# A planner with pauses: steps fed by another engine drawn behind a set amount of other work, k times v one step later, queries ahead of the spreading

## The chip, the cores and the metric

One core of one Trainium2 chip runs the whole program. The metric is the device time of one launch in microseconds (us). Before the change it is 5066.79 us, the median of 3 runs (5059.32 to 5072.86).

## The reference

The input is x, 8 images of 384 channels on 32 by 32 pixels, all in fp32. Four layers follow one another; only the first two are touched by the change.

```python
# layer 0, per image; both directions of the sequence of 1024 pixels
xn   = rmsnorm(x)                              # over the 384 channels
u, z = split(xn @ in_proj)                     # 384 -> 768
u    = silu(conv1d(u))                         # 4 taps, depthwise
dt, B, C = split(u @ x_proj)                   # 24, 16, 16
delta = softplus(dt @ dt_proj + b)
h[t] = exp(delta*A)*h[t-1] + delta*u*B         # 384 channels x 16 states
y    = (sum_n h*C + u*D) * silu(z)
x1   = x + 0.5*(0.25*(fwd + bwd) @ out_proj + sigmoid(dwconv3x3(xn))*xn)
# layer 1, per image
h = c2(bn2(dwconv3x3(c1(bn1(x1))))) + x1       # c1, c2: 384 -> 384
q, k, v = split(qkv(h)); phi(t) = exp(0.5*(2t - t*t))
out = phi(q) @ (phi(k)^T v) / (phi(q) . sum phi(k))   # 8 heads of 48
h = h + proj(out)
x2 = h + mlp(layernorm(h))                     # 384 -> 1536 -> 384
# layer 2: seven depthwise convolutions (sum); layer 3: 1x1, 13x13 depthwise, gelu
```

## The kernel before, in words

**Stages.** An image is 1024 pixels in two halves of 512, with channels in NC = 3 groups of 128 partitions. For an image b there are three routines. `front(b)` makes what the scan reads: the norm (squares, a mean over channels by matmul `ms_s`, a reciprocal root `ms_r` on ScalarE, its spreading over partitions by matmul `ms_b`, the product `xn` on VectorE), the input projection `in` with weights `win`, the 3x3 gate `lc`, the 1-d convolution `c`, then `xd` and `dt`. `scan(b)` is the recurrence. `layer1(b)` is the output projection `op` and all of layer 1: `h`, `dw`, `c2`, k and v with their product `kvs`, the key sum and its spreading (`kss`, `kvp`), queries `q`, denominator `den` with its reciprocal `rz` and the spreading `rzb`, projection `pj`, layernorm (`mu`, `var_s`, `var_r`, `var_b`) and the MLP (`mf`, `mo`). At the end of all images come the two 13x13 convolutions with a pointwise product between (L330, L376), which the change does not touch.

**The scan.** It has 48 rounds in an image: 12 units (direction, half, channel group) of NR = 4. In each round ScalarE makes four exponentials `da` (L846), VectorE two products `du` (L851) and four recurrences `hs` (L863), GpSimd two products with C (L872), and TensorE sums the result with four matmuls into `acc` (L552 and L557, the line of a helper that all column-tiled products share). `hs` has 8 buffers, two a round, so VectorE may be four rounds ahead of TensorE; `da` has 4. The eight scans run one after the other, and the other two routines are dealt out between the rounds: while image b is scanned, `layer1(b-1)` and `front(b+1)` are.

**What sets the order.** Each routine is a Python generator that issues some instructions and yields the cost of what it just issued, about the TensorE time in us. A planner (L1194 to L1221) keeps a list of jobs [generator, total cost, first round, last round, cost done]. After each scan round it draws from the job that is furthest behind an even pace until none is behind. `front(b)` counts 100 units, paced from 8 rounds before the end of the scan two images earlier to 9 before the end of the last one; `layer1(b)` counts 310 over the 48 rounds of the next image. The order in which the program is written gives the priority; a scheduler then orders each engine's instructions by it[...]. Steps with a `defer` come one or more draws later (L527). Two helpers, `together` and `col32` (L547, L559), keep groups of matmuls together.

**Where the steps are written.** `front`: xi loads L639, squares L643, `rsqrt_mean` (L608) and `spread_rows` (L622), xn L650, win L658, t3 (the taps of lc) L673, lc L678, conv1d L707, xd L718, dt L736. `layer1`: kvs L1025, the k/v projections L1011, kv L1030, kss L1040, kvp L1054, wq L1061, q L1072, den L1080, rz L1085 to L1087, rzb L1092, pj L1098, mu L1106, var L1113 to L1132, MLP L1153 to L1180. Pools that matter: PSUM "mm" (`psum`) has 2 buffers, "mo" (`long_psum`) 3; `t2` 9, `a6` 7, weights `w` 4, images of rows `im` 8 in SBUF.

Of the kernel before, what the change touches and what calls it, by code (L numbers as in the profile page):

```python
# [11 lines left out]
AF = mybir.ActivationFunctionType  # L12
# [4 lines left out]
P = 128  # L17
# [390 lines left out]
def _layers01(tc, nc, B, xv, x2_d, dram, ident, mean_w, eps5, eps6, one, half, minus1, vec, bns, bnt,  # L408
# [12 lines left out]
    with ExitStack() as ctx:  # L421
# [84 lines left out]
        def t2(name):  # L506
            return sp.tile([P, HALF], FP, tag="t2", name=name, bufs=N_T2)
# [61 lines left out]
        def rows(t):  # L569
            return t.rearrange("p (h w) -> p h w", w=W)  # L570
# [51 lines left out]
        def spread_rows(r, name):  # L622
            ps = psum(f"{name}_b")
            for j in range(4):
                nc.tensor.matmul(
                    ps[:, j * P : (j + 1) * P], spread[:, j, :], r, start=True, stop=True,
                    skip_group_check=True,
                )
            return ps
# [2 lines left out]

        def front(b):

            xn = []
            for h in range(2):
                cols = bass.ts(h, HALF)
                xh = a6(f"xi_{b}_{h}")
                nc.sync.dma_start(xh, xv[b][:, :, cols])  # L639
                yield 0  # L640
                sqs = [t2(f"sq_{b}_{c}_{h}") for c in range(NC)]
                for c in range(NC):
                    nc.scalar.activation(sqs[c], xh[:, c, :], AF.Square)  # L643
                yield 0
                r = rsqrt_mean(sqs, eps6, f"ms_{b}_{h}")
                yield 1
                rstd = spread_rows(r, f"ms_{b}_{h}")
                t, mid = image6(f"xn_{b}_{h}")
                for c in range(NC):
                    nc.vector.scalar_tensor_tensor(  # L650
                        mid[c], rows(xh[:, c, :]), vec("norm_w", c), rows(rstd), ALU.mult, ALU.mult
                    )
                put_image(xn_d, b % 2, h, t, nc.gpsimd)
                xn.append(mid)
                yield 2
            uo = u_d[b % 2].rearrange("(c p) i -> p c i", p=P)
            for e in range(2):
                w = wtile(inproj_t[:, e * C : (e + 1) * C], f"win_{b}_{e}")  # L658
                for h in range(2):
                    for m in range(NC):  # L660
                        ps = psum(f"in_{b}_{e}_{m}_{h}")
                        dense(ps, w, m, xn[h])
                        t = t2(f"uz_{b}_{e}_{h}_{m}")
                        if e == 0:
                            nc.scalar.copy(t, ps)
                            nc.scalar.dma_start(uo[:, m, 3 + h * HALF : 3 + (h + 1) * HALF], t)
                        else:
                            nc.scalar.activation(t, ps, AF.Silu)
                            nc.scalar.dma_start(zv[b][:, m, bass.ts(h, HALF)], t)
                        yield 3  # L670


            t3 = tapw(taps3, f"t3_{b}")  # L673
            for h in range(2):
                for c in range(NC):
                    xr = t2(f"xr_{b}_{h}_{c}")
                    nc.sync.dma_start(xr, xv[b][:, c, bass.ts(h, HALF)])
                    ps = conv3(rows3(xn_d, b % 2, h, c, f"lc_{b}_{h}_{c}"), c, t3, f"lc_{b}_{h}_{c}")  # L678
                    lc = t2(f"lg_{b}_{c}_{h}")
                    nc.scalar.activation(lc, ps, AF.Tanh, bias=dwh[:, c, :], scale=0.5)  # L680

                    def local(h=h, c=c, lc=lc, xr=xr):
                        nc.vector.scalar_tensor_tensor(
                            rows(lc), rows(lc), one, xn[h][c], ALU.add, ALU.mult
                        )
                        nc.vector.scalar_tensor_tensor(xr, lc, rsh, xr, ALU.mult, ALU.add)
                        nc.gpsimd.dma_start(x1v[b][:, c, bass.ts(h, HALF)], xr)

                    defer(1, local)
                    yield 3  # L690


            for h in range(2):
# [33 lines left out]
                for d in range(2):  # L727
                    lo = 64 * d + DTR
                    nc.scalar.dma_start(bc_d[b, d][:, cols], xd[lo : lo + 2 * NST, :])
                yield 3  # L730
                for c in range(NC):
                    dls = []
                    for d in range(2):
# [209 lines left out]
        def layer1(b):  # L943
# [43 lines left out]
            for h in range(2):  # L987
# [13 lines left out]
                kvs[: PR + 1, 0:C], zero[:, 0 : PR + 1], zero[:, 0:C], start=True, stop=False,  # L1001
                skip_group_check=True,
            )
            for t in range(L // P):
                h, q = divmod(t, HALF // P)
                pix = xx[h][:, :, q * P : (q + 1) * P]
                kp, vt = t2(f"kp_{b}_{t}"), t2(f"vt_{b}_{t}")
                for w, dst in ((wk, kp), (wv, vt)):
                    ps = psum(f"kv_{b}_{t}_{dst.name}")
                    for k in range(NC):  # L1010
                        nc.tensor.matmul(  # L1011
                            ps[:, :C], pix[:, k, :], w[:, k, :], start=(k == 0), stop=(k == NC - 1)
                        )
                    if w is wk:
                        phi(kp[:, :C], ps[:, :C], f"k_{b}_{t}")
                    else:
                        vv1 = vt[:, : C + NPR].rearrange("p (a e) -> p a e", e=PR + 1)
                        nc.scalar.copy(vv1[:, :, PR : PR + 1], ones)
                        nc.scalar.copy(
                            vv1[:, :, 0:PR], ps[:, :C].rearrange("p (a e) -> p a e", e=PR)  # L1020
                        )
                last = t == L // P - 1
                for a in range(NPR):
                    s = slice(a * PR, (a + 1) * PR)
                    nc.tensor.matmul(  # L1025
                        kvs[: PR + 1, s], vv1[:, a, :], kp[:, s], start=False, stop=last,
                        skip_group_check=True,
                    )
                yield 6
            kv = t2(f"kv_{b}")  # L1030
            nc.vector.tensor_mul(
                kv[:PR, :C].rearrange("p (a e) -> p a e", e=PR),
# [2 lines left out]
            )  # L1035

            nc.scalar.copy(kv[PR : PR + 1, :C], kvs[PR : PR + 1, :C])
            kss = psum(f"kss_{b}")
            for c in range(NC):
                nc.tensor.matmul(  # L1040
# [12 lines left out]
            for a in range(NPR):  # L1053
# [4 lines left out]
                t = t2(f"kvp_{b}_{a}")  # L1058
                nc.scalar.copy(t[:PR, :C], ps[:PR, :C])
                nc.scalar.dma_start(kvp_d[b % 2, a * PR : (a + 1) * PR, :], t[:PR, :C])  # L1060
            wq = wtile(qkv_t[:, 0:C], f"wq_{b}")  # L1061
            kvp = wtile(kvp_d[b % 2], f"kvw_{b}")
            yield 4


            qps, xns = [], []
            for h in range(2):
                qp = a6(f"qp_{b}_{h}")
                qps.append(qp)
                for m in range(NC):  # L1070
                    ps = long_psum(f"q_{b}_{h}_{m}")
                    dense(ps, wq, m, xx[h])  # L1072
                    phi(qp[:, m, :], ps, f"q_{b}_{h}_{m}")
                    yield 3

            den, rz = long_psum(f"den_{b}"), t2(f"rz_{b}")
            ats = [slice(32, 64), slice(96, 128)]
# [7 lines left out]
                nc.scalar.activation(rz[at, :], den[at, :], AF.Ln, bias=eps6[at])  # L1085
            for at in ats:
                nc.scalar.activation(rz[at, :], rz[at, :], AF.Exp, scale=-1.0)  # L1087
            yield 3
            for k in range(NC):
                for h, at in enumerate(ats):  # L1090
                    ps = long_psum(f"rzb_{b}_{h}_{k}")
# [29 lines left out]
                    nc.vector.tensor_mul(xns[h][:, k, :], xns[h][:, k, :], rstd)  # L1121

            sq = squares(0)
            yield 0
            r0 = rsqrt_mean(sq, eps5, f"var_{b}_0")
            sq = squares(1)
            yield 1
            r1 = rsqrt_mean(sq, eps5, f"var_{b}_1")
            scaled(0, r0)
            yield 3  # L1130
            scaled(1, r1)
            yield 2  # L1132

            behind_gelu = []

# [55 lines left out]
        seconds = [layer1(b) for b in range(B)]  # L1191


        jobs = [[fold(), 36, 0, rounds, 0], [prepare, 7, 0, rounds, 0]]  # L1194
        for b in range(1, B):
            jobs.append([front(b), 100, max(0, (b - 1) * rounds - 8), b * rounds - 8 - 1, 0])
        for b in range(B - 1):
            jobs.append([seconds[b], 310, (b + 1) * rounds + 0, (b + 2) * rounds + 0, 0])
        for b in range(B):
            for i, _ in enumerate(scan(b)):  # L1200
                tick()
                if i == rounds:
                    break
                at = b * rounds + i
                if i == rounds - 8:
                    next(seconds[b])

                while True:
                    due = [
                        (w[4] / w[1] - (at + 1 - w[2]) / (w[3] - w[2]) if at + 1 < w[3] else -1, n)  # L1210
                        for n, w in enumerate(jobs) if w[2] <= at
                    ]
                    if not due or min(due)[0] >= 0:
                        break
                    w = jobs[min(due)[1]]
                    cost = next(w[0], None)
                    if cost is None:
                        jobs.remove(w)
                    else:
                        w[4] += cost  # L1220
        tick(everything=True)  # L1221

        scan_ctx.close()
# [95 lines left out]
```

## Time and profile before

| what | value |
|---|---|
| time, median of 3 runs | 5066.79 us (5059.32 to 5072.86) |
| span of the profiled execution | 5036.6 us |
| mean granted clock of TensorE | 0.906 |
| TensorE busy | 4203.6 us, 83% of the span |
| VectorE busy | 3791.7 us, 75% |
| GpSimd busy | 2997.3 us, 60% |
| ScalarE busy | 2637.3 us, 52% |
| front(0) alone | 0 to about 147 us |
| scans of images 0 to 7 begin | 150.8, 674.5, 1160.9, 1662.6, 2165.5, 2666.5, 3165.4, 3653.3 us |
| last scan ends | 4087.9 us |
| layer1(7) alone, with the windows' loads | to about 4490 us |
| convolutions and the product between | to 5036.6 us |

The page gives no other time of the profiled execution than its span, 30.2 us below the median of the runs. Times of engines are sums of instruction durations in that one execution. [...] In the views of waits a line reads "who waited for whom: us in all, times, longest"; in the views of windows, each row is a stretch of the span with the busy time and count of every engine, the granted clock, the share of the DMA engines and GB/s. "acc k" below is the sum of scan round k, counted from 0 in each image; what lies between acc k and acc k+1 in TensorE's list is what the other two routines do there.

### The profile page before, as it was taken

To read this page: it belongs to the slowest core of one execution; us is meant where nothing else is said; L and a number is where in the kernel's file an instruction comes from. 1 tells how busy PE (TensorE), PEld (TensorE's weight loads), DVE (VectorE), ACT (ScalarE), POOL (GpSimd) and SP (SyncE) were. 2 spreads that over 40 slices of the span, in tenths; PEclk is the share of its full clock that TensorE was granted. 3 is DMA by queue.
4 is the path that set the end of the run, shared out by engine and by line. 5 is a ranking of instruction groups with operands and counts; after the bars stand their busy time and mean duration, and the time that the engine had idled before them with its cause. 6 is when DMAs were issued, how large, how long until landed. Compare 5 with 4: busy or idle time off the path is not lost. (4 is left out here: it accounts for less than half of the span.)

```text
span 5036.6 us, 58480 instructions
## 1 busy us (share of the span) xinstructions
PE 4203.6 (83%) x20128; PEld 1781.9 (35%) x20128; DVE 3791.7 (75%) x3861; ACT 2637.3 (52%) x3738; POOL 2997.3 (60%) x1546
## 2 busy tenths in 40 slices
PE   6466588888888888889888989889888879978988
PEld 2121223333333233323332333333333324457457
DVE  1599999878987898789978997889898830157256
ACT  2456555774577457745774577567645622200212
POOL 1477577666766676667666666766776760033058
PEclk9676799899989998999899989998988989999999
DMA  7976557577657765776577657765763672389798
GB/s 205 278 226 221 182 190 214 179 216 195 214 175 214 196 213 174 213 195 214 177 214 191 216 179 212 210 214 180 176 192 127 160 156 78 68 162 251 210 207 172
DMA packets 543120, 965.28 MB, mean 192 GB/s; under 512 B 56568, under 2 KB 220904, under 8 KB 542824
## 3 DMA queue, kind: packets, MB, share of 16 engines
q1 hardware_dynamic: 401648, 663.89, 45.1%
q0 software_dynamic: 58048, 205.76, 15.8%
q10 hardware_dynamic: 83128, 91.90, 6.7%
q8 instruction: 159, 2.61, 0.2%
q14 instruction: 137, 1.12, 0.1%
HBM read 726.36 MB, written 234.98 MB: 191 GB/s over the span
## 5 line engine op out<-in xcount | busy, mean ns | idle before, releaser
L872 POOL TENSOR_TENSOR hs<-hs,bct 128x1024 f32<-128x1024 f32 x768 | 2414.6, 3145 | 945.5 <-DVE carry L868 438.6
L846 ACT ACTIVATE da<-dlt,neg_a 128x512 f32<-128x512 f32 x1536 | 1035.8, 715 | 1041.4 <-DVE hs L863 970.7
L863 DVE TENSOR_TENSOR_SCAN hs<-da,carry,du 128x512 f32<-128x512 f32 x768 | 942.4, 1266 | 191.8 <-PE acc L557 139.1
L851 DVE TENSOR_TENSOR du<-vr,bct 128x1024 f32<-128x1024 f32 x768 | 1033.0, 1345 | 31.4 <-DMA vr<-v_d 19.6
L863 DVE TENSOR_TENSOR_SCAN hs<-da,du 128x512 f32<-128x512 f32 x768 | 900.9, 1208 | 129.3 <-PE acc L557 54.4
L557 PE MATMUL acc<-hs,selt 128*32 128x512 f32 x2304 | 541.5, 660 | 134.8 <-POOL hs L872 134.7
L539 PE MATMUL mf<-ln,w 128*128 128x512 f32 x1152 | 549.2, 623 | 27.6 <-DMA w<-w_d 17.0
L1172 PE MATMUL mo<-hm,w 128*128 128x512 f32 x1152 | 532.7, 600 | 15.0 <-DVE xx L1139 15.0
L552 PE MATMUL acc<-hs,selt 128*32 128x512 f32 x768 | 420.9, 643 | 58.6 <-POOL hs L872 50.3
L539 PE MATMUL in<-xn,win 128*128 128x512 f32 x576 | 292.4, 646 | 64.6 <-DMA win<-in_inproj_t 29.0
L539 PEld LDWEIGHTS mf<-ln,w 128*128 128x128 f32 x1152 | 222.8, 200 | 339.4 <-issue 271.9
L1172 PEld LDWEIGHTS mo<-hm,w 128*128 128x128 f32 x1152 | 214.5, 190 | 309.1 <-issue 281.3
L846 ACT ACT_TABLE_LOAD x235 | 301.5, 1283 | 7.1 <-DMA dw_i<-h_d 2.4
L330 PE MATMUL cv_a<-xt_a,tp_a 128*32 128x256 f32 x3072 | 183.8, 387 | 55.1 <-issue 26.6
L1142 POOL DMA_DIRECT2D x_d<-xx x48 | 56.5, 1179 | 282.1 <-DVE xx L1139 274.9
L539 PE MATMUL op<-g,wo 128*128 128x512 f32 x288 | 158.3, 701 | 73.8 <-DMA g<-g_d 73.8
L557 PE MATMUL dw<-dw_i,t3b 96*32 96x512 f32 x1056 | 203.9, 637 | 16.5 <-DMA dw_i<-h_d 16.1
L330 PE MATMUL cv_b<-xt_b,tp_b 128*32 128x256 f32 x3072 | 184.5, 393 | 38.3 <-DVE xt_b L306 25.7
L306 DVE COPY xt_b<-xt_b 32x2496 f32<-32x2496 f32 x96 | 149.2, 1554 | 68.0 <-DMA xt_b<-xp_d 63.4
L539 PEld LDWEIGHTS in<-xn,win 128*128 128x128 f32 x576 | 111.6, 204 | 237.1 <-issue 165.0
L330 PEld LDWEIGHTS cv_a<-xt_a,tp_a 128*32 128x32 f32 x3072 | 159.6, 138 | 79.6 <-issue 34.7
L330 PEld LDWEIGHTS cv_b<-xt_b,tp_b 128*32 128x32 f32 x3072 | 155.7, 139 | 67.4 <-issue 41.1
(196 smaller groups left out, 5758.8 us busy)
## 6 DMA issues: line engine op xcount, KB each, us to landing
dlt<-dl_d SPq DMA_DIRECT2D x384, 256.0 KB, 4.6
vr<-v_d SPq DMA_DIRECT2D x384, 256.0 KB, 5.0
bct<-bc_d SPq DMA_DIRECT2D x256, 256.0 KB, 3.9
ut<-u_d SPq DMA_DIRECT2D x192, 257.5 KB, 5.7
lc_i<-xn_d SPq DMA_DIRECT2D x192, 228.8 KB, 5.4
dw_i<-h_d SPq DMA_DIRECT2D x192, 228.8 KB, 5.4
w<-w_d SPq DMA_DIRECT2D x64, 576.0 KB, 6.1
w<-in_w SPq DMA_DIRECT2D x64, 576.0 KB, 5.7
```

The costliest lines, as they stand in the source:

```text
L306: nc.vector.tensor_copy(xt[at[e] : at[e] + e * H, :, 0 : RL - e - (e - 1)], xt[at[0] : at[0] + e * H, :, e : RL - (e - 1)],)
L330: nc.tensor.matmul(ps[H * e : H * (e + 1), 0:BW], tp[:, c, :].rearrange("p (j t) -> p j t", t=KT)[:, :, t], rhs, start=(t == 0), stop=(t = ...
L539: product = nc.tensor.matmul(ps, w[:, k, m * P : (m + 1) * P], rhs[k] if isinstance(rhs, list) else rhs[:, k, :], start=(k == 0), stop=(k ...
L552: first = product()
L557: tc.keep_in_program_order(product())
L846: nc.scalar.activation(da[:, bass.ts(j, HALF)], dlt[:, bass.ts(j, HALF)], AF.Exp, scale=neg_a[:, g, r : r + 1],)
L851: nc.vector.tensor_mul(pairs(du), pairs(vt), bct[r][:, 0:1, :].to_broadcast([P, 2, HALF]),)
L863: nc.vector.tensor_tensor_scan(t[:, s][:, way], da[:, s][:, way], du[:, s][:, way], k_c if second else 0.0, ALU.mult, ALU.add,)
L872: made.append(nc.gpsimd.tensor_mul(pairs(t), pairs(t), bct[r][:, 1:2, :].to_broadcast([P, 2, HALF])))
L1142: nc.gpsimd.dma_start(x2v[m, :, h * (H // 2) : (h + 1) * (H // 2), PADW + b * (W + PADW) : PADW + b * (W + PADW) + W,], rows(o),)
L1172: nc.tensor.matmul(acc[m], wb[:, f, m * P : (m + 1) * P], hm, start=(i == 0 and f == 0), stop=(i == FF // C - 1 and f == NC - 1),)
```

## The change

Three things change; the instructions are the same in number and kind.

- **The planner** counts what it has issued, one for each scan round and the cost of each draw. A routine may yield (cost, pause): it isn't drawn again until so many units of other work have been issued, except when its last round is reached.
- **`front`**: both halves' xi are loaded first. The steps of the norm are pipelined over the halves, with pauses of 8, 6, 6, 6 and 4 units; win_0, win_1 and t3 are loaded earlier; the rows of each lc are loaded 3 units before the convolution; 4 units stand after xd.
- **`layer1`**: the kvs matmuls of step t are drawn after the projections of step t+1; the first three queries stand before and behind the last kvs and ahead of kss and kvp, and wq's load with them; 3 units stand before den, 6 after it, and 6, 6, 6, 3 around the steps of the layernorm.

```diff
         def front(b):
-            xn = []
+            xn, xhs, rs_h = [], [], {}
             for h in range(2):
-                cols = bass.ts(h, HALF)
                 xh = a6(f"xi_{b}_{h}")
-                nc.sync.dma_start(xh, xv[b][:, :, cols])
-                yield 0
...
+                nc.sync.dma_start(xh, xv[b][:, :, bass.ts(h, HALF)])
+                xhs.append(xh)
+            yield 0, 8
...
+            sqs = square(0)
+            yield 0, 6
+            rs_h[0] = rsqrt_mean(sqs, eps6, f"ms_{b}_0")
+            sqs = square(1)
+            yield 1, 6
+            normed(0)
+            rs_h[1] = rsqrt_mean(sqs, eps6, f"ms_{b}_1")
+            win = wtile(inproj_t[:, 0:C], f"win_{b}_0")
+            yield 3, 6
+            normed(1)
+            yield 2, 4
             uo = u_d[b % 2].rearrange("(c p) i -> p c i", p=P)
             for e in range(2):
-                w = wtile(inproj_t[:, e * C : (e + 1) * C], f"win_{b}_{e}")
+                w = win
                 for h in range(2):
+                    if e == 0 and h == 1:
+                        win = wtile(inproj_t[:, C : 2 * C], f"win_{b}_1")
+                    if e == 1 and h == 1:
+                        t3 = tapw(taps3, f"t3_{b}")
...
-                    ps = conv3(rows3(xn_d, b % 2, h, c, f"lc_{b}_{h}_{c}"), c, t3, f"lc_{b}_{h}_{c}")
+                    ims = rows3(xn_d, b % 2, h, c, f"lc_{b}_{h}_{c}")
+                    yield 0, 3
+                    ps = conv3(ims, c, t3, f"lc_{b}_{h}_{c}")
...
-                yield 3
+                yield 3, 4
                 for c in range(NC):
@@ layer1
+            behind_kv = []
             for t in range(L // P):
...
+                if behind_kv:
+                    behind_kv.pop()()
+                behind_kv.append(summed)
                 yield 6
+            wq = wtile(qkv_t[:, 0:C], f"wq_{b}")
...
+            qps.append(a6(f"qp_{b}_0"))
+            queries(0, 0)
+            yield 3
+            behind_kv.pop()()
             kv = t2(f"kv_{b}")
...
+            queries(0, 1)
+            yield 3
+            queries(0, 2)
+            yield 3
             kss = psum(f"kss_{b}")
...
-            wq = wtile(qkv_t[:, 0:C], f"wq_{b}")
             kvp = wtile(kvp_d[b % 2], f"kvw_{b}")
             yield 4
...
+            qps.append(a6(f"qp_{b}_1"))
+            for m in range(NC):
+                queries(1, m)
+                yield 3
+            yield 0, 3
 
             den, rz = long_psum(f"den_{b}"), t2(f"rz_{b}")
...
-            yield 3
+            yield 3, 6
             for k in range(NC):
                 for h, at in enumerate(ats):
                     ps = long_psum(f"rzb_{b}_{h}_{k}")
...
             sq = squares(0)
-            yield 0
+            yield 0, 6
             r0 = rsqrt_mean(sq, eps5, f"var_{b}_0")
             sq = squares(1)
-            yield 1
+            yield 1, 6
             r1 = rsqrt_mean(sq, eps5, f"var_{b}_1")
             scaled(0, r0)
-            yield 3
+            yield 3, 6
             scaled(1, r1)
-            yield 2
+            yield 2, 3
@@ planner
+                issued[0] += 1
                 while True:
-                    due = [
-                        (w[4] / w[1] - (at + 1 - w[2]) / (w[3] - w[2]) if at + 1 < w[3] else -1, n)
-                        for n, w in enumerate(jobs) if w[2] <= at
-                    ]
-                    if not due or min(due)[0] >= 0:
+                    due = []
+                    for n, w in enumerate(jobs):
+                        if w[2] > at:
+                            continue
+                        late_by = w[4] / w[1] - (at + 1 - w[2]) / (w[3] - w[2]) if at + 1 < w[3] else -1
+                        if late_by < 0 and (w[5] <= issued[0] or at + 1 >= w[3]):
+                            due.append((late_by, n))
+                    if not due:
                         break
                     w = jobs[min(due)[1]]
                     cost = next(w[0], None)
                     if cost is None:
                         jobs.remove(w)
                     else:
+                        cost, pause = cost if isinstance(cost, tuple) else (cost, 0)
                         w[4] += cost
+                        issued[0] += cost
+                        w[5] = issued[0] + pause
```

`summed` is the block of kvs matmuls of one step, `queries(h, m)` one query product with its phi, and `square`, `normed` the two halves of the old norm loop; their instructions are those of before.

More of the change, by code (lines that the diff above doesn't have):

```diff
@@ L633, in front, with square, normed @@
         def front(b):
-            xn = []
+            xn, xhs, rs_h = [], [], {}
             for h in range(2):
-                cols = bass.ts(h, HALF)
                 xh = a6(f"xi_{b}_{h}")
-                nc.sync.dma_start(xh, xv[b][:, :, cols])
-                yield 0
+                nc.sync.dma_start(xh, xv[b][:, :, bass.ts(h, HALF)])
+                xhs.append(xh)
+            yield 0, 8
+            def square(h):
                 sqs = [t2(f"sq_{b}_{c}_{h}") for c in range(NC)]
                 for c in range(NC):
-                    nc.scalar.activation(sqs[c], xh[:, c, :], AF.Square)
-                yield 0
-                r = rsqrt_mean(sqs, eps6, f"ms_{b}_{h}")
-                yield 1
-                rstd = spread_rows(r, f"ms_{b}_{h}")
+                    nc.scalar.activation(sqs[c], xhs[h][:, c, :], AF.Square)
+                return sqs
+            def normed(h):
+                rstd = spread_rows(rs_h[h], f"ms_{b}_{h}")
                 t, mid = image6(f"xn_{b}_{h}")
@@ L650, in front @@
                     nc.vector.scalar_tensor_tensor(
-                        mid[c], rows(xh[:, c, :]), vec("norm_w", c), rows(rstd), ALU.mult, ALU.mult
+                        mid[c], rows(xhs[h][:, c, :]), vec("norm_w", c), rows(rstd), ALU.mult, ALU.mult
                     )
@@ L670, in front @@
                         yield 3
-            t3 = tapw(taps3, f"t3_{b}")
             for h in range(2):
@@ L1021, in layer1, with summed, queries @@
                         )
[L1022 to L1028, printed above, removed]
-                yield 6
+                def summed(t=t, vv1=vv1, kp=kp):
+                    for a in range(NPR):
+                        s = slice(a * PR, (a + 1) * PR)
+                        nc.tensor.matmul(
+                            kvs[: PR + 1, s], vv1[:, a, :], kp[:, s], start=False, stop=t == L // P - 1,
+                            skip_group_check=True,
+                        )
+                if behind_kv:
+                    behind_kv.pop()()
+                behind_kv.append(summed)
+                yield 6
+            wq = wtile(qkv_t[:, 0:C], f"wq_{b}")
+            qps, xns = [], []
+            def queries(h, m):
+                ps = long_psum(f"q_{b}_{h}_{m}")
+                dense(ps, wq, m, xx[h])
+                phi(qps[h][:, m, :], ps, f"q_{b}_{h}_{m}")
+            qps.append(a6(f"qp_{b}_0"))
+            queries(0, 0)
+            yield 3
+            behind_kv.pop()()
             kv = t2(f"kv_{b}")
@@ L1060, in layer1 @@
                 nc.scalar.dma_start(kvp_d[b % 2, a * PR : (a + 1) * PR, :], t[:PR, :C])
-            wq = wtile(qkv_t[:, 0:C], f"wq_{b}")
             kvp = wtile(kvp_d[b % 2], f"kvw_{b}")
             yield 4
[L1066 to L1073, printed above, removed]
-                    yield 3
+            qps.append(a6(f"qp_{b}_1"))
[3 more added lines that the diff above has]
+            yield 0, 3
             den, rz = long_psum(f"den_{b}"), t2(f"rz_{b}")
@@ L1123, in layer1 @@
             sq = squares(0)
-            yield 0
+            yield 0, 6
             r0 = rsqrt_mean(sq, eps5, f"var_{b}_0")
             sq = squares(1)
-            yield 1
+            yield 1, 6
             r1 = rsqrt_mean(sq, eps5, f"var_{b}_1")
             scaled(0, r0)
-            yield 3
+            yield 3, 6
             scaled(1, r1)
-            yield 2
+            yield 2, 3
             behind_gelu = []
@@ L1191, in _layers01 @@
         seconds = [layer1(b) for b in range(B)]
-        jobs = [[fold(), 36, 0, rounds, 0], [prepare, 7, 0, rounds, 0]]
+        issued = [0]
+        jobs = [[fold(), 36, 0, rounds, 0, 0], [prepare, 7, 0, rounds, 0, 0]]
         for b in range(1, B):
-            jobs.append([front(b), 100, max(0, (b - 1) * rounds - 8), b * rounds - 8 - 1, 0])
+            jobs.append([front(b), 100, max(0, (b - 1) * rounds - 8), b * rounds - 8 - 1, 0, 0])
         for b in range(B - 1):
-            jobs.append([seconds[b], 310, (b + 1) * rounds + 0, (b + 2) * rounds + 0, 0])
+            jobs.append([seconds[b], 310, (b + 1) * rounds + 0, (b + 2) * rounds + 0, 0, 0])
         for b in range(B):
```

## The prediction

> **What bounds the kernel now.** I read the page first (busy shares, slices), then busy time by window for the images, then TensorE's waits over five images, then the windows of one image between its scan sums. Most of the time is eight scans of 435 to 524 us each. [...] Busy time of images 2 to 6, from the windows view (us, then each engine's busy us and count, granted clock, DMA share, GB/s):
> ```profile
> 1160.00:1662.00 502.00, 444.97 (x1698) 168.91 (x1697) 425.45 (x424) 324.16 (x449) 332.43 (x148) 0.94 0.68 200
> 1662.00:2165.00 503.00, 443.99 (x1698) 168.47 (x1697) 425.48 (x423) 323.04 (x447) 333.72 (x149) 0.94 0.68 199
> 2165.00:2666.00 501.00, 442.16 (x1697) 169.31 (x1696) 422.82 (x423) 323.00 (x447) 332.30 (x149) 0.94 0.68 200
> ```
> TensorE is busy 88%, VectorE 85%, GpSimd and ScalarE 65%. Two engines are near full, so a TensorE wait costs only where VectorE isn't late as well. TensorE's waits from 1131 to 3591 us (total, times, longest):
> ```profile
> PE op L539 <- DMA g<-g_d: 43.0, 5, 10.9
> PE acc L557 <- POOL hs L872: 30.2, 13, 2.8
> PE kvs L1025 <- ACT vt L1019: 26.6, 25, 2.1
> PE var_s L613 <- ACT vs L1115: 24.7, 10, 4.5
> PE in L539 <- DMA win<-in_inproj_t: 19.3, 4, 5.0
> PE rzb L1092 <- ACT rz L1087: 18.0, 5, 3.9
> PE ms_b L625 <- ACT ms_r L619: 14.3, 4, 4.5
> ...
> PE kss L1040 <- ACT kv L1037: 10.2, 5, 2.1
> PE ms_s L613 <- ACT sq L643: 9.5, 4, 3.2
> PE lc L552 <- DMA t<-in_taps: 7.9, 4, 2.1
> ```
> The change aims at all of these but op and acc: 26.6+24.7+19.3+18.0+14.3+10.2+9.5+7.9 = 130.5 us, 26 an image. Image 3, cut at acc 5, 20, 24, 31, 32 and 34, shows where they can count:
> ```profile
> 1663.00:1721.00 58.00, 49.12 (x128) 18.79 (x127) 50.16 (x56) 25.09 (x37) 38.61 (x17) 0.93 0.64 174
> 1721.00:1888.00 167.00, 152.11 (x748) 57.90 (x752) 147.66 (x135) 98.19 (x158) 116.63 (x42) 0.99 0.74 226
> 1888.00:1928.00 40.00, 36.10 (x108) 13.43 (x100) 32.39 (x39) 29.67 (x39) 21.65 (x10) 0.87 0.60 212
> 1928.00:1986.00 58.00, 44.94 (x200) 15.70 (x200) 53.75 (x62) 39.63 (x51) 35.35 (x21) 0.82 0.44 148
> 1986.00:2022.00 36.00, 36.00 (x114) 13.88 (x106) 31.70 (x35) 35.26 (x44) 28.12 (x13) 1.00 0.64 207
> 2022.00:2158.00 136.00, 120.75 (x403) 47.16 (x402) 103.62 (x92) 92.05 (x117) 88.79 (x46) 0.94 0.72 197
> ```
> Stage A (to acc 20) and C (after acc 31) are TensorE's: hs is ready 20 to 39 us before its acc. In B (1928:1986) VectorE is busy 53.75 of 58 and TensorE 44.94, and acc 28, 29 and 31 come within 4 us of their hs.
>
> [...] in image 3 the 3.9 us gap ahead of rzb and the 4.46 ahead of var_s are each followed by 10.2 us of records at clock 0.5. [...] Images 2 to 6 hold 59 to 65 us at 0.5 each[...]. [...]
>
> **Part by part.** Instruction counts and durations stay; only order and waits move. The compiled orders of both kernels were weighed with before's durations (dense matmul 0.875 us, acc round 1.0, row convolution 2.9): 404.8 us of TensorE work an image in both.
>
> *Start.* xi_1 is issued at 14.4 us, behind win and t3 on SP, and ScalarE's squares wait 15.5 us for it. Both xi now go first. in begins at 39.2; its chain behind xi_1's squares shortens by about that wait less some queueing: −14 (bounds −20 to −5). SP's win and t3 go later by two issues of 0.43 us, hidden under the norms.
>
> *A: k times v a step later, queries ahead, lc's rows early.* Each kvs now has the next step's k and v projections (4.0 us) or more ahead of it, so vt's wait of at most 2.1 goes: 26.6/5 = 5.3; kss has two queries ahead (2.0), lc's taps come early (1.6). A few slots of PSUM will be waited for instead (two "mm" buffers, kvs still open): 2.5 back. [...] Sum: −8 an image (−10 to −2), all on the path, since hs waits there for acc. The SP loads moved (wq, kvp, rows) pass no load of the scan that is due within 20 us. Six images: −48.
>
> *B: pauses in layer1.* rzb is drawn 6 units after den, but the compiled order still has only acc 23 and xd_0 between them (3.7 us), against four activations of ScalarE for rz: wait kept. var_s falls behind acc 25 to 27 and two conv1d; that wait of 4.9 goes, but those accs wait for VectorE, so TensorE is late at acc instead: 0. The price is elsewhere: layer1 is held some ten rounds and then catches up. From acc 20 to acc 33 the new order holds 65 us of TensorE work (before: 113), and between acc 33 and acc 34 stand 58.2 us of MLP with no acc (before: longest 35.6, after acc 31). In before, acc 31 comes 98.6 us after acc 20, on hs's heels. hs 33 is two rounds on; VectorE spends 425/48 = 8.8 us a round: 116, less some 6 of qp's wait for rzb (20.9/5 = 4.2) and similar = 110, plus GpSimd's 3.1 and 0.5: acc 33 at 114. Then 1 + 58[...] gives acc 34 at 175, against 154.3 (1887.7 to 2042.0). +20 an image, six images: +120. Bounds: if VectorE ran through at 8.8 from its 24 us lead, hs 33 were ready at 90, acc 34 at 155: 0; if it keeps all its waits and the pauses delay xd_1, +30.
>
> *C: the norm of the next image.* ms_s, ms_b and in get 9 us of MLP or an acc round between steps: 14.3 + 9.5 over four ends is 6, win 4.8[...]; together 19. hs is 28 to 39 us ahead there until round 43, but −3.8 at round 47, where VectorE binds: I take −16 (−19 to 0), 5.5 ends: −88.
>
> *Image 7.* layer1(6) alone, its pauses now worth up to 6 rounds each: rounds 23 to 45 are light (5 to 7 us of TensorE a round), then 52.6 us of MLP between acc 45 and 46: +9 (−5 to +20). *Image 1* takes 12.2 us of TensorE work over from image 0 (order: 399.6 to 411.8), which is VectorE-bound at clock 0.5: +12 (0 to 12). Stages after the scans hold the same order; layer1(7) alone has gaps at rzb 3.5 and var 4.3 only: 0. The op waits (43.0/5) are untouched.
>
> *Sum:* −14 − 48 + 120 − 88 + 9 + 12 = −9. The profiled execution spans 5036.6; the runs have a median of 5066.79, 30.2 above, which I take to stay. 5036.6 − 9 + 30.2 = 5058.
>
> **Rivals.**
> 1. *The burst is hidden* (B costs 0): VectorE gains from earlier ln and no waits, reaches hs 33 at 90 us. Then −9 − 120 = −129: 4938. For: VectorE idles 78 us an image. Against: its lead at rounds 28 to 31 is nil now, so it has no slack exactly there.
> 2. *The burst eats C's gain too.* hs has buffers for four rounds ahead: during the 59 us VectorE can do 4×8.8 = 35 and stands 24 us. If it then can't recover, the rounds after acc 38 wait for hs, and removing ms and win waits returns nothing: +88 on the sum, 5146. It decides when one wait of hs for acc exceeds 20 us and acc waits for hs in rounds 40 to 47. For: round 47 is VectorE's already. Against: hs starts C four full rounds ahead.
> 3. *The change doesn't do what it says*: the scheduler reorders by priority and the measured order is as before: 5067.
>
> **Chances.** About 0.3% (15 us) is what a measurement of this kernel can tell from no change. Forecast's case 0.45: its terms' bounds give ±40 around 5058, so 0.15 faster, 0.16 within, 0.14 slower. Rival 1 0.24, all faster; rival 2 0.26, all slower; rival 3 0.05, within. Faster 0.39, within 0.21, slower 0.40. The range reaches into both: 4955 to 5140; the likeliest case alone is 5018 to 5098.
>
> **What would show it.** Right: kvs and kss gone from TensorE's waits, var_s replaced by acc, a hs wait for acc of over 15 us after acc 33 in every image, the stretch acc 20 to 34 longer by 10 to 30, acc 34 to 47 shorter by about 16, sq's 15.5 us wait at the start gone. Wrong: acc 34 at under 160 us after acc 20, or kvs waits turned into waits for PSUM of the same size, or a new DMA wait in the burst for w.

## The result and the profile after

The changed kernel takes 5231.98 us (median of 4 runs, 5227.02 to 5241.17) against 5069.82 us before (now of 4 runs, 5059.32 to 5076.28): ratio 1.0323, 95% interval 1.0306 to 1.0339. The forecast was 5058, 9 us under before, with a range of 4955 to 5140. The kernel came out 162 us slower, above that range. The profiled execution after spans 5225.3 us, 6.7 under its median; that of before spans 5036.6, 33 under. The stages below therefore add up to 188.7, not to the 162 of the medians.

Busy time of images 2 to 4 after (windows from acc 0 to the next image's acc 0; columns as before):
```profile
1207.00:1728.80 521.80, 452.80 (x1697) 172.20 (x1696) 421.27 (x423) 320.43 (x444) 332.53 (x149) 0.91 0.65 192
1728.80:2254.20 525.40, 454.60 (x1697) 173.22 (x1696) 423.06 (x423) 320.36 (x444) 332.09 (x149) 0.90 0.67 191
2254.20:2779.30 525.10, 453.67 (x1697) 175.00 (x1696) 421.27 (x423) 320.11 (x444) 332.17 (x149) 0.91 0.65 191
```
The same 1697 matmul records take 453 to 455 us instead of 442 to 445, at clock 0.90 to 0.91 instead of 0.94, and an image is 20 to 24 us longer. (In both profiles TensorE's clock is 1 or 0.5 at any time, with 107 stretches at 0.5 before and 120 after. What that means for a record: in image 3 before, mf's last 592 ns at clock 1, in the median, and 1061 to 1222 at 0.5.) VectorE has the same work and is less full: nothing was added, more is waited for. TensorE's waits after, over five images:
```profile
PE acc L557 <- POOL hs L890: 77.7, 35, 3.2
PE acc L552 <- POOL hs L890: 46.6, 25, 3.9
PE kvp L1094 <- ACT lg L698: 25.7, 5, 5.2
PE mf L539 <- DMA w<-w_d: 23.2, 4, 6.5
PE kv_vt L1030 <- DMA wv<-in_qkv_t: 18.6, 4, 5.6
...
PE kvp L1094 <- DVE ks L1085: 12.7, 5, 2.6
...
PE rzb L1124 <- ACT rz L1119: 9.4, 5, 1.9
...
PE var_s L613 <- ACT uc L730: 7.9, 5, 1.6
```
VectorE's, from the same stretch:
```profile
DVE hs L881 <- PE acc L557: 199.8, 45, 16.8
DVE ud L763 <- PE mo L1204: 71.3, 5, 14.6
...
DVE qp L1125 <- PE rzb L1124: 34.8, 5, 7.0
```
kvs, kss, win, ms_b and ms_s are gone from TensorE's waits as meant, rzb's wait is halved, var_s's fell from 24.7 to 7.9. In their place stand acc (124.3 instead of 41.8), kvp, w and wv. Image 3 by stage: first before, cut at its own acc 8, 20, 34 and 48, then after.
```profile
1690.70:1768.10 77.40, 74.25 (x308) 24.30 (x307) 66.45 (x76) 49.12 (x68) 56.55 (x18) 1.00 0.76 228
1768.10:1887.70 119.60, 106.61 (x533) 44.16 (x533) 110.19 (x93) 67.53 (x116) 84.69 (x32) 0.99 0.69 213
1887.70:2042.00 154.30, 137.34 (x476) 50.71 (x472) 132.58 (x146) 124.64 (x157) 98.49 (x49) 0.90 0.56 189
2042.00:2196.00 154.00, 124.80 (x394) 49.01 (x392) 114.74 (x109) 81.71 (x108) 92.82 (x52) 0.90 0.74 181
```
```profile
1728.80:1803.70 74.90, 74.43 (x305) 24.54 (x304) 64.87 (x73) 47.91 (x66) 55.26 (x18) 1.00 0.78 233
1803.70:1930.40 126.70, 109.14 (x527) 46.00 (x527) 108.73 (x93) 70.03 (x116) 85.75 (x32) 0.92 0.66 204
1930.40:2109.20 178.80, 147.26 (x477) 53.90 (x473) 127.46 (x146) 121.72 (x155) 97.94 (x48) 0.85 0.51 167
2109.20:2254.00 144.80, 123.57 (x394) 48.78 (x392) 121.93 (x111) 80.70 (x108) 92.94 (x52) 0.91 0.81 187
```
The third row of each, acc 20 to 34, holds the main loss: 24.5 us. acc 33 comes 114.4 us after acc 20 (forecast: 114), and acc 34 only 64.4 later. Here is the stretch from acc 24 to acc 33 before, then the same after, then acc 33 to 34 after:
```profile
1928.10:2032.10 104.00, 90.94 (x340) 33.41 (x340) 92.72 (x102) 84.89 (x106) 68.98 (x36) 0.90 0.54 182
```
```profile
1969.20:2044.80 75.60, 49.48 (x224) 14.96 (x222) 65.25 (x77) 59.54 (x76) 47.21 (x28) 0.75 0.43 142
2044.80:2109.20 64.40, 61.62 (x142) 25.37 (x142) 32.87 (x34) 34.82 (x43) 31.65 (x14) 0.95 0.52 166
```
From acc 24 to 33 TensorE now has too little to do: 26 us idle, at clock 0.75. In the burst of MLP work that follows it is nearly full, 61.62 of 64.4 us, and VectorE stands for half of it, busy 32.87. In the second row of the stages, acc 8 to 20, the time should have become shorter and is 7.1 us longer, at clock 0.92 instead of 0.99.

The forecast's sum, term by term, against the stages of the two traces (us; images 1 to 6 in A, B and C):

| term | forecast | measured |
|---|---|---|
| start, to the first acc | −14 | −6 |
| image 0 | −8 (its part of C) | +4 |
| A, to acc 20 | −48 | +33 |
| B, acc 20 to 34 | +120 | +148 |
| C, acc 34 to 48 | −80 | −43 |
| image 1's share of front | +12 | within A; not seen by itself (image 1 is 19.9 longer, images 2 to 4 are 20 to 24). Image 0 before, to which the forecast gave clock 0.5, has 0.71 over its 523 us, with VectorE busy 470.75 |
| image 7 | +9 | +24 |
| layer1(7) and the convolutions | 0 | +28 |
| sum | −9 | +188 |

### The profile page after: what moved, and what is told of

Same layout as the page of the kernel before. It is cut to its first block, busy times and chain, and to the rows that moved or that the text cites. A ratio compares the mean times of both kernels' runs of the same rounds, so it can differ in the third digit from the quotient of the medians.

```text
span 5225.3 us, 58347 instructions
## 1 busy us (share of the span) xinstructions
PE 4279.7 (82%) x20128; PEld 1809.5 (35%) x20128; DVE 3759.9 (72%) x3861; ACT 2596.0 (50%) x3700; POOL 2999.4 (57%) x1546
## 5 line engine op out<-in xcount | busy, mean ns | idle before, releaser
L869 DVE TENSOR_TENSOR du<-vr,bct 128x1024 f32<-128x1024 f32 x768 | 1013.9, 1320 | 33.3 <-DMA vr<-v_d 21.1
L557 PE MATMUL acc<-hs,selt 128*32 128x512 f32 x2304 | 610.4, 677 | 218.1 <-POOL hs L890 218.0
L539 PE MATMUL mf<-ln,w 128*128 128x512 f32 x1152 | 570.3, 643 | 46.1 <-DMA w<-w_d 31.5
L552 PE MATMUL acc<-hs,selt 128*32 128x512 f32 x768 | 434.4, 660 | 132.6 <-POOL hs L890 96.7
L539 PE MATMUL in<-xn,win 128*128 128x512 f32 x576 | 274.2, 617 | 21.5 <-ACT uz L682 9.6
L552 ACT ACTIVATE hm<-mf,biasf 128x512 f32<-128x512 f32 x128 | 88.0, 688 | 271.7 <-PE mf L539 270.8
L330 PE MATMUL cv_b<-xt_b,tp_b 128*32 128x256 f32 x3072 | 185.0, 395 | 36.5 <-DVE xt_b L306 23.4
L557 PEld LDWEIGHTS acc<-hs,selt 128*32 128x32 f32 x2304 | 94.9, 114 | 345.7 <-POOL hs L890 330.8
L552 PEld LDWEIGHTS acc<-hs,selt 128*32 128x32 f32 x768 | 65.2, 113 | 388.2 <-issue 200.9
```

Of the source, the lines that this page charges most:

```text
L330: nc.tensor.matmul(ps[H * e : H * (e + 1), 0:BW], tp[:, c, :].rearrange("p (j t) -> p j t", t=KT)[:, :, t], rhs, start=(t == 0), stop=(t = ...
L539: product = nc.tensor.matmul(ps, w[:, k, m * P : (m + 1) * P], rhs[k] if isinstance(rhs, list) else rhs[:, k, :], start=(k == 0), stop=(k ...
L552: first = product()
L557: tc.keep_in_program_order(product())
L869: nc.vector.tensor_mul(pairs(du), pairs(vt), bct[r][:, 0:1, :].to_broadcast([P, 2, HALF]),)
```

## The experiments

Two accounts of the result were on trial. Theory P: layer1's pauses empty the rounds after acc 20, and that is the loss of B and image 7; stage A lost because early weights and the close kss and kvp made a few long waits of many short ones. Rival W: early weights in front keep layer1's weights out of their four buffers, and that is the loss everywhere. The runs were on several chips (the kernel before took 5023 to 5050 us in them), so times are given as ratios to before on the same chip, and stages by their length. The first four expectations give times in us; before took 5023 on their chip, 47 less than in the result, so these times can't be compared as they stand. This table collects the means over images 1 to 5: length of the stage, in brackets TensorE's time without a matmul, and the time at clock 0.5. Part of the time at 0.5 passes while TensorE waits anyway: 13 of 67 us an image in before.

| kernel | A, to acc 20 | B, acc 20 to 34 | C, acc 34 to 48 | ratio (95%) |
|---|---|---|---|---|
| before | 197.8 (15.8, 9.6) | 154.0 (16.6, 30.0) | 151.2 (26.3, 27.3) | 1 |
| changed | 203.3 (19.0, 19.8) | 178.7 (31.6, 53.9) | 142.6 (19.3, 23.9) | 1.0323 |
| l1_pause_only | 197.6 (16.7, 11.9) | 185.0 (40.7, 58.0) | 147.3 (22.6, 24.6) | 1.0430 (1.0417–1.0444) |
| no_l1_pause | 204.9 (20.0, 22.5) | 153.9 (19.5, 25.3) | 138.0 (17.1, 19.1) | 0.9983 (0.9975–0.9992) |
| front_only | 205.3 (18.5, 16.2) | 154.1 (17.2, 33.6) | 138.8 (17.9, 19.1) | 0.9986 (0.9977–0.9995) |
| kv_only | 205.3 (20.7, 23.5) | 151.7 (14.3, 25.3) | 149.5 (24.7, 24.6) | 1.0066 (1.0052–1.0079) |
| capped12 | 200.7 (16.0, 18.4) | 155.0 (36.8, 53.2) | 159.1 (14.4, 14.3) | 1.0281 (1.0262–1.0301) |
| t3_late | 201.5 (18.8, 15.0) | 154.3 (18.9, 28.7) | 137.8 (17.6, 17.7) | 0.9941 (0.9929–0.9953) |
| far_t3_late | 196.8 (20.3, 13.0) | 159.8 (15.8, 25.9) | 139.3 (18.4, 18.4) | 0.9912 (0.9898–0.9926) |
| before_again | 197.9 (15.2, 12.7) | 154.0 (16.3, 29.4) | 148.6 (24.5, 23.2) | one run |
| var_pause | 201.2 (18.2, 15.0) | 180.3 (36.6, 55.3) | 144.6 (20.6, 24.6) | 1.0318 (1.0298–1.0339) |
| rzb_pause | 201.2 (18.3, 14.3) | 156.6 (17.2, 28.0) | 143.1 (22.1, 21.8) | 0.9985 (0.9975–0.9995) |
| kvp_mo | 199.9 (17.5, 13.7) | 151.4 (16.8, 23.9) | 143.1 (21.6, 22.5) | 0.9902 (0.9885–0.9919) |
| front_t3_win1_late | 203.2 (15.9, 17.1) | 154.3 (18.3, 30.0) | 143.2 (21.2, 23.2) | 0.9956 (0.9940–0.9972) |

**The parts alone.** First layer1's six pauses in the kernel before, with the new planner:
```diff
+            yield 0, 3
+
             den, rz = long_psum(f"den_{b}"), t2(f"rz_{b}")
...
-            yield 3
+            yield 3, 6
...                                    # and four more around the layernorm
```


> The kernel before with the new planner and the six pauses in layer1 alone. Its compiled order has 57 us of TensorE work between acc 33 and acc 34 and, in image 7, 53 us between acc 45 and 46, as the changed kernel. Theory P (the pauses make the burst, and the burst is the loss): acc 20 to 34 is longer by 22 to 28 us an image, image 7 and what follows it by 30 to 45 us; stages A and C as before; time about 5230 to 5260. Rival W (the loss is that weights loaded earlier in front keep layer1's weights out of their four buffers): the burst alone costs under 8 us an image, time under 5140.

Measured 1.0430: B +31.0 us an image, more than the 22 to 28 expected; image 7 454.6 us (before 432.2, in before_again 425.5), and it and what follows together 41 longer, as expected. About 2 us of B's growth is den's work, which the pause ahead of den moves there from A (486 matmul records instead of 476 in B). Theory P holds and W falls: no weight was moved here. Its image 3, stages A, B and C:
```profile
1740.80:1936.10 195.30, 178.77 (x823) 68.50 (x822) 176.73 (x168) 116.20 (x184) 140.77 (x49) 0.98 0.72 221
1936.10:2120.30 184.20, 144.31 (x486) 52.28 (x482) 132.66 (x146) 116.83 (x150) 97.58 (x49) 0.84 0.48 164
2120.30:2269.00 148.70, 125.26 (x394) 49.16 (x392) 115.78 (x109) 81.20 (x107) 92.57 (x51) 0.91 0.71 181
```
Of the three stages B alone is hurt: 184.20 us at clock 0.84.

The reverse, the changed kernel with `yield 0`, `3`, `0`, `1`, `3`, `2` at those six places:

> The changed kernel without the six pauses in layer1; the front and the k, v and query order stay changed. Theory P: acc 20 to 34 falls back to 152 to 158 us an image, image 7 to 430 to 436; stage A keeps its +5 an image, C its -9 and the start its -6; time 5030 to 5065. Rival W: the burst goes but the loss stays, acc 20 to 34 over 165 us or new waits for w elsewhere; time over 5130.

Measured 0.9983, 5016.45 us: 0.2% under before, less than the 0.3% that the prediction took as noise. B is back at 153.9, within 152 to 158, and the start keeps its 6. Image 7 at 427.5 is below the expected 430 to 436, C at −13.2 gained more than the 9 and A at +7.1 lost more than the 5. Rival W's 165 us in B and 5130 in all are far off. Image 3:
```profile
1672.40:1875.80 203.40, 183.91 (x831) 70.55 (x831) 175.26 (x168) 118.81 (x184) 142.17 (x49) 0.95 0.69 213
1875.80:2028.90 153.10, 133.75 (x477) 51.44 (x473) 133.61 (x146) 124.67 (x156) 97.06 (x48) 0.92 0.56 189
2028.90:2168.90 140.00, 121.00 (x394) 47.44 (x392) 121.37 (x111) 84.46 (x113) 93.61 (x53) 0.93 0.79 200
```
The two other parts, each alone in the kernel before: the new `front` with the planner, and the new order of k times v and queries without any pause.

> The kernel before with the new planner and the new front alone. If the early load of t3 is what makes wv late, kv_vt's wait of 4 to 5 us for the DMA of wv is here, stage A is about 5 us longer less 2 for lc, and kvp has no wait for ScalarE; C is 8 to 10 us shorter an image, with mf's wait of 6 us for w in it; the start is 6 shorter. Time 5010 to 5050. If wv's wait comes from layer1's own new order, it isn't here and the time is 4990 to 5020.

> The kernel before with layer1's new order of k times v and queries alone; no pauses, the old front. If this order itself makes kvp wait (kss and kvp now lie close together behind the last kvs), kvs's 5.3 and kss's 2 us go and kvp's 7.6 us come: stage A within 3 us of before, time 5050 to 5085. If kvp's wait comes from front's lc placed ahead of it, stage A is 6 to 9 us shorter an image, time 5010 to 5030.

front_only is 0.9986: C −12.4 and the first acc 7.2 earlier, both a little more than expected, but A +7.5 where some 3 were expected, with kv_vt's wait of up to 5.0 for the DMA of wv. kv_only is 1.0066: A is also +7.5, outside both of its expectations. kvs's waits went, and kss (5.6 at most) and kvp (2.4) wait instead. So each part makes A longer by itself, with different waits, and both together by no more (+7.1).

**Is the burst the loss, or the light rounds before it?** The planner stops drawing at about 12 units a round, except in an image's last three rounds; the pauses are kept:
```diff
                 issued[0] += 1
-                while True:
+                upto = issued[0] + 12
+                while issued[0] < upto or at % rounds > rounds - 4:
```


> The changed kernel with all pauses, but the planner draws at most some 12 units after a scan round, so that the 58 us between acc 33 and 34 become 32 and the rest 11 to 17 a round up to acc 38. Theory L (the loss is TensorE's idle time and low clock in the light rounds before the burst: from acc 20 to 33 there are 65 us of work for 114, and the rest has to be done later in any case): acc 20 to 34 is shorter, but acc 20 to 48 stays within 8 us of the changed kernel's 321; time 1.025 to 1.036 of before. Theory D (the burst itself is the loss, because VectorE stands 24 us in it): acc 20 to 48 falls by 15 us or more an image; time under 1.018.

Measured 1.0281. acc 20 to 48 is 314.1 us on the mean, 7.2 under the changed kernel's 321.3, and 22.2 over the 291.9 of no_l1_pause. Theory L, that the light rounds are the loss, holds, near the edge of what it allowed; D, that the burst is, falls. The cap doesn't take the burst away altogether: in image 3 acc 34 comes 38.7 us after acc 33 (64.4 without the cap; before's longest stretch between two accs is 37.6). Image 7 isn't cured at all, since its burst lies in the last three rounds: 60.8 us from acc 45 to 46, image 7 449.4. Stages B and C of image 3:
```profile
1911.60:2067.40 155.80, 119.49 (x416) 42.68 (x412) 133.66 (x146) 112.58 (x146) 95.79 (x46) 0.81 0.50 172
2067.40:2231.20 163.80, 147.16 (x455) 58.88 (x454) 118.01 (x112) 96.08 (x123) 94.10 (x54) 0.94 0.72 184
```
B now looks cured, 155.80, but only 416 of its 477 matmul records are in it; 36 us are idle and the clock is 0.81. The rest is paid for in C, 163.80. A stage must be read with the count of what it did.

Which pauses: both variants stand on t3_late, below.

> The run with t3 late, with the four pauses around the layernorm of layer1 put back and those before and after den left out. Its order has 49 us of TensorE work between acc 32 and 33, and in image 7 46 us between acc 45 and 46. If these four pauses are what empties rounds 24 to 32: acc 20 to 34 is 172 to 182 us an image (154 without), image 7 and what follows 30 to 45 us longer; time 1.020 to 1.032 of before. If the one after den matters as much, acc 20 to 34 is under 166 and the time under 1.012.

> The run with t3 late, with only the pause of 6 between den and rzb put back. Its order differs in images 1 to 6 by one row convolution or less. acc 20 to 34 stays within 3 us of 154; rzb's wait of 4 us falls by no more than 2. In image 7 the planner's rounds 23 to 28 change: within 6 us. Time 0.990 to 0.998 of before. If a single pause already makes the loss, over 1.005.

The four pauses around the layernorm make the whole of it: B 180.3 (t3_late 154.3), image 7 and what follows 40 longer, ratio 1.0318, all as expected. The one after den makes no burst: B 156.6, and rzb's wait stays at 16.2 us in four images, as in t3_late. Its ratio, 0.9985, lies 0.0005 above what was expected; C was 143 in the three kernels on that chip without the layernorm's pauses, against 138 on the chip of t3_late, with longer waits of mf for its weights (33.4 to 38.2 us in four images, against 25.1), so the pause needn't be the cause.

**Why stage A lost.** TensorE's waits in stage A of image 3, before and then after:
```profile
PE kvs L1025 <- ACT vt L1019: 6.3, 5, 2.1
PE dw L557 <- DMA dw_i<-h_d: 2.2, 3, 1.4
PE lc L552 <- DMA t<-in_taps: 2.1, 1, 2.1
PE kss L1040 <- ACT kv L1037: 2.0, 1, 2.0
```
```profile
PE kvp L1094 <- ACT lg L698: 5.1, 1, 5.1
PE kv_vt L1030 <- DMA wv<-in_qkv_t: 4.3, 1, 4.3
PE kvp L1094 <- DVE ks L1085: 2.5, 1, 2.5
```
Many waits of at most 2.1 us became few of 2.5 to 5.1. Over images 1 to 5 TensorE's idle time in A grows by 3.2 us and its busy time, with nearly the same matmuls, by 2.3, while the time at half clock doubles (9.6 to 19.8). wv's cause is in SyncE's queue, before and then after:
```profile
1755.64 0.59 SPq L517 DMA_DIRECT2D wk<-in_qkv_t  x1
1757.01 0.38 SPq L517 DMA_DIRECT2D wv<-in_qkv_t  x1
```
```profile
1792.08 0.55 SPq L517 DMA_DIRECT2D wk<-in_qkv_t  x1
...
1813.37 0.53 SPq L517 DMA_DIRECT2D wv<-in_qkv_t  x1
```
wv was issued 1.4 us behind wk and is now 21.3 behind it. t3, the taps, shares the four weight buffers, and takes its buffer earlier; wv may have had to wait for one. So t3 goes back, on top of no_l1_pause:
```diff
-                    if e == 1 and h == 1:
-                        t3 = tapw(taps3, f"t3_{b}")
...
+            t3 = tapw(taps3, f"t3_{b}")
             for h in range(2):
```


> The changed kernel without the pauses in layer1, and with t3 loaded where it was before. If t3 in one of the four weight buffers is what holds wv back, kv_vt's wait for the DMA of wv (4.2 us) goes and stage A is 4 to 7 us an image shorter than without the move (205): 198 to 201; time 0.990 to 0.994 of before. If wv is held by win or by SP's order, the wait stays and the time is 0.998.

wv's wait is gone and wv is again issued 0.7 us behind wk, so t3's early load was the cause; that it acts by the buffer is argued, as SyncE issues other loads in the 21 us between. A falls from 204.9 to 201.5, by 3.4 where 4 to 7 were expected, and the ratio is 0.9941, at the upper end of what was expected. What is left in A is above all kvp's wait, and ScalarE's timeline in the changed kernel says where it is from (columns: start, us, engine, line, operation; idle before, and what ended it):
```profile
1893.44 0.72 ACT L864 ACTIVATE da<-dlt,neg_a 128x512 f32<-128x512 f32 x1 [5.13 <-DVE hs L881]
1894.07 0.67 ACT L958 ACTIVATE phi_q<-q,minus 128x512 f32<-128x512 f32 x1
...
1897.76 1.33 ACT L864 ACTIVATE da<-dlt,neg_a 128x512 f32<-128x512 f32 x2 [0.72 <-DVE hs L881]
...
1901.58 1.33 ACT L864 ACTIVATE da<-dlt,neg_a 128x512 f32<-128x512 f32 x2 [1.02 <-DVE hs L881]
1902.82 0.67 ACT L698 ACTIVATE lg<-lc,dwh 128x512 f32<-128x512 f32 x1
```
lc's last matmul ended at 1893.9, and its PSUM buffer is read at 1902.82, 9 us later. In between ScalarE works for 6.6 us on activations that stand ahead in its queue, and waits 2.3 us for VectorE (0.60 for kv, in a row not shown, 0.72 and 1.02 for hs). kvp takes that buffer and starts at 1903.54. So the reading had its input 9 us before its turn on ScalarE came. kvp's second wait, for ks of VectorE, fits the other mm buffer, the one of kss, which ks reads. Two trials followed. kss and kvp behind one more query:
```diff
             queries(0, 2)
             yield 3
+            qps.append(a6(f"qp_{b}_1"))
+            queries(1, 0)
+            yield 3
             kss = psum(f"kss_{b}")
```


> As the run with t3 late, and kss and kvp are drawn behind the fourth query. If kvp's 5.1 and 2.5 us are ScalarE's and VectorE's delay in reading kv and kss, one more query and two convolutions cover it: stage A at 190 to 195 us, time 0.980 to 0.986 of before. If they are a wait for a PSUM buffer, which moves with them, stage A stays at 198 to 201, time 0.990 to 0.994.

Then kss and kvp in the other PSUM pool (`kss = long_psum(...)`, `ps = long_psum(...)`), back in their place:

> The run with t3 late, with kss and the four kvp in the PSUM pool of three buffers (mo) instead of the one of two (mm). If kvp's wait of 5.2 us is for a mm buffer that ScalarE has not read, it goes or falls under 2 us and stage A is 4 to 9 us shorter than the 201.5 of the run with t3 late; time 0.983 to 0.990. If it is the delay of kv itself on ScalarE, or queries hold mo as long, the wait stays under another name and stage A within 3 us of 201.5.

The waits of both, far_t3_late first, over four images:
```profile
PE kss L1081 <- ACT uc L729: 19.7, 4, 4.9
...
PE kvp L1096 <- DMA pj<-in_proj_t: 14.4, 4, 3.9
```
```profile
PE kvp L1093 <- ACT phi_q L957: 25.2, 8, 5.6
```
In both the wait only changes its name: kss now waits for ScalarE to read the conv1d's buffer, or kvp for it to read a query's. far_t3_late has A at 196.8, between its two expectations, but this is no gain: 42 of A's 833 matmul records, most of them the conv1d's, now come after acc 20, and B is 5.5 longer. A and B together are 356.6 us against 355.8 in t3_late. Its ratio 0.9912 is that of the rival, and pj's load now comes late too; why it lies below t3_late's 0.9941 the stages don't show (its profile is of the slowest of six executions, t3_late's of the fastest). kvp_mo has A within 3 us of t3_late, as its rival said, and 0.9902, just above the range of its first case: A 1.6 and B 2.9 shorter are 27 us in six images, of which the ratio shows 20, but it ran on another chip, where C is 5.3 longer. These two are the fastest kernels seen, and can't be told from each other.

> The new front and planner with layer1 as before, t3 and win_1 loaded where they were before, win_0 early. If win_1's early load holds a buffer that the MLP's weights need, mf's wait of 6 to 7 us for the DMA of w in the norm stage goes and acc 34 to 48 falls from 137.8 to 129 to 134 us; if in then waits for win_1 instead, it stays at 136 to 140. With layer1's old order stage A has kvs's waits and no kvp wait: 196 to 203. Time 0.984 to 0.993 of before.

Missed in every number: mf's wait for w stays, 33.4 us in four images (up to 9.4), though win_1 is late, so it isn't win_1 alone. C at 143.2 lies outside both forecasts and is as in the other kernels on that chip; A at 203.2 and the ratio of 0.9956 are just above theirs. Whether win_0's buffer is the cause wasn't tried.

> The kernel before, profiled on this chip, as the base of the stages: stage A about 195 us, acc 20 to 34 about 154, acc 34 to 48 about 151, with a time within 0.5% of before.

5018.78 us, 0.1% under before's median on that chip. Its stages A, B and C agree with those of the first profile within 3 us an image, so that base is sound to that; image 7 is 6.7 shorter.

## Why the prediction was wrong

Take the pauses of layer1 apart from the rest. Without them the forecast's own terms add up to −138 us (start −14, A −48, C −88, image 1 +12); no_l1_pause measured 0.2% under before, less than 10 us. The pauses were put at +129 (B +120, image 7 +9); they cost 1.0323 less 0.9983, some 170. So most of the miss lies in gains that didn't come, and there in A, and a lesser part in the price of the pauses.

*A is the largest miss: −48 forecast, +33 measured.* Its first half was right: kvs, kss and lc's taps lost their waits (8.9 us an image). The step that failed is "A few slots of PSUM will be waited for instead [...]: 2.5 back": that term measured 7.7 an image at kvp alone (25.7 + 12.7 over five), since a reading waits for its turn on ScalarE (9 us in image 3). It is the sign that the prediction itself had named, kvs waits turned into waits for PSUM. It failed again at "The SP loads moved [...] pass no load of the scan that is due within 20 us": the load that came late was not the scan's. t3's early load held wv back, 3.7 us an image (18.6/5). And the waits that it lists add up to −6.4; the rest of its −8 was the author's estimate for the clock, where TensorE was busy 2.3 longer. By these lists idle time changes by −8.9 + 7.7 + 3.7 = +2.5, where the stage shows +3.2; with 2.3 busy that is the +5.5 an image that was measured.

*The clock* was read half right. After rzb's 3.9 us gap in image 3 before, the half clock lasts 10.2 us although TensorE doesn't idle in them. The 10.2 us at var_s begin inside the gap, and only 6.2 us of records fall in them. Of the 67 us at 0.5 in an image before, TensorE works in 54 (means of images 1 to 5), so the other 13 can't count as slowed work. What the half clock costs beside the waits was the author's estimate wherever the forecast has it.

*B was right in mechanism and near in size:* +20 forecast, +24.7 an image. acc 33 came at 114.4, and acc 34 at 178.8 instead of 175 (the 2 us of it beyond 114 + 1 + 58 were the author's estimate). TensorE is idle 15.0 longer and busy 9.7 longer with the same matmuls, at half clock for 23.9 us more. That acc 33 fits to 0.4 us is in part luck: the sum took off 6 us for qp's wait for rzb and similar, and that wait grew from 4.2 to 7.0 an image. The stall came as foreseen, in each of images 1 to 6: ud waits some 14 us for mo, and hs 16.8 for acc 34, with 15 named as a sign and 20 as the point where rival 2 was to decide. C still gained, and acc waits for hs in rounds 46 and 47 alone, as before. But the stall is not what the time goes on: of the 29 us that the pauses cost in B and C (321.3 less 291.9) the cap saves 7 by cutting the burst; 22 remain, and are put down to the light rounds, where the trace has TensorE idle; light rounds with no burst at all weren't run. Rival 1, a hidden burst, is refuted, and so is rival 3, since the order changed as meant.

*C:* −16 an image forecast, −8.6 measured, −13.2 in no_l1_pause. The waits named went; "9 us of MLP [...] between steps" was right. Those waits are 10.8 of the 19 that the forecast began from; the rest was the author's estimate for the clock. A new wait of mf for w, 5.8 an image (23.2/4), was missed, and the pauses took another 4.6.

*Image 7 and its tail:* +9 forecast, +24 measured, and then +28 where "Stages after the scans hold the same order [...]: 0" was forecast. That was wrong: the pauses left the second half of the op products behind the last acc, and layer1(7)'s h begins 16.4 us later after the scan. 8.6 more stand between the MLP's end and the first convolution (33.0 instead of 24.4); why wasn't looked into. l1_pause_only has image 7's loss as well, no_l1_pause does not.

*The start:* in began 10.8 us earlier, but the first acc only 6.0: ScalarE's copies of u waited 10.5 us for DMAs of earlier ones, instead of 2.0. "some queueing" was priced too low.

## What to carry to other kernels

A pause by counted work is only as good as the work that fills it: where the other jobs are few, it empties the rounds of an engine that has no spare time later (26 us of TensorE idle here from acc 24 to 33). When a wait is removed by an early load or by an order, follow the buffer that it takes and the queue of the engine that must give it back. From acc 8 to 20 of image 3, with waits of up to 2.1 us, TensorE's mean clock was 0.99 and 533 matmul records took 106.61 us; with single waits of 4.3 and 5.1 us it was 0.92, and 527 took 109.14. Here the long waits came with a cost beyond their length.

## What the runs showed that was not expected

The same matmuls took 2.6 us longer in stage A of kv_only than in before, on top of 4.9 us more idle time: the half clock went from 9.6 to 23.5 us. How much of this comes from the length of the waits (kss 5.6 at most, where before's longest in image 3 is 2.1) and how much from their sum wasn't tried apart. And two parts that each cost 7.5 us in A cost 7.1 together.

A stage's length can mislead in both directions: capped12's B and far_t3_late's A look short because work has left them.
